# Attention block on one core: the places of the bias additions, of the weight split's test, of the residual loads and of the range test

## The chip, the cores and the metric

The kernel runs on one core of a Trainium2 chip. The metric is the time of one execution on the device in microseconds (us). A core has five engines, each with an instruction queue of its own that it works through in order: TensorE (PE in a profile, with its weight loads apart as PEld), VectorE (DVE), ScalarE (ACT), GpSimd (POOL) and SyncE (SP), which here only issues DMAs.

## The reference

```python
def reference(x, gn_scale, gn_bias, qkv_w, qkv_b, proj_w, proj_b):   # x: (4, 512, 48, 48) float32
    hn = group_norm(x, 32 groups) * gn_scale + gn_bias
    qkv = einsum('oc,bchw->bohw', qkv_w, hn) + qkv_b
    q, k, v = qkv as float16, 8 heads of 64 channels, 2304 positions
    w = softmax(einsum('bhct,bhcs->bhts', q * s, k * s))             # s = 64 ** -0.25 in float16
    a = einsum('bhts,bhcs->bhct', w, v)
    return x + einsum('oc,bchw->bohw', proj_w, a) + proj_b
```

## The kernel before

The function `fast_path` does the whole computation. A general version follows it behind a flag, and runs only if the sums of the softmax left a safe range or if the split of the projection weights was not exact; with these inputs it does not run. All engines' orders are written out by hand: the Python code emits instructions in exactly the order in which each engine's queue holds them.

Heads are worked on in pairs, 4 pairs for each of 4 images, 16 pairs `g` in all. Positions of the queries fall into 5 blocks `j`, four of 512 and one of 256. The list `stream` cuts this into 432 bursts, 27 for a pair (6, 6, 6, 6, 3 for the blocks). The main loop `for n in range(end)` emits burst `n`:

- `prepare(n)`: SP's transfers for the bias additions (below).
- `scores`: six matmuls into three two-bank tiles `ps`, and an `Exp` of ScalarE on each, which writes the tile `p`.
- `add(stream[n-1])`: VectorE adds the `p` of the burst before to the float16 sum `acc`. At the last burst of a block two or three smaller additions, the joins (L1184), fold `acc` together.
- `values(stream[n-BEHIND])`: matmuls of `v` with the `p` of two bursts ago into `av`; at a block's end VectorE copies `av` out (`avx`).
- `fill(n)`: work beside the attention. It runs VectorE tasks from the deque `tasks` (statistics `st` and normalization L776 of the next image) up to a budget `room`, and then pieces from the list `beside`: chains of matmuls that make `q`, `k` (tile `pqk`), `v` (`pv`) and the output projection (`pr`). A chain comes whole or in two halves in two bursts. One PSUM bank (`pw`) serves all chains, so that a chain begins once VectorE has copied the chain before out of it (L833, L882, L1032). The first chain on the next image's `v` waits in the list until block 0 of that image has been normalized in an earlier burst (`when`).

After a block's end at burst `e`, the sums are added up over partitions by PE (`sl`, L1207, into the bank that `av` had) at `e+3` and copied out (`slx`), inverted at `e+4` (`invert`), spread by DMA through DRAM at `e+5` (`spread`: `row`, `ib`), and multiplied with `avx` on POOL at `e+6` (`divide`, L1275). `check_sums` is the range test, four small operations of POOL on the sums at the end of a pair.

Four parts lie outside these chains:

- Bias additions. `fetch_x` loads a piece of `x` (256 KB, two buffers `pre`), `add_bias` adds the projection's bias on POOL two bursts later at the earliest (L946), `keep_biased` stores the piece in DRAM (`xb`) one burst after that. There are 72 pieces. `prepare` fetches one every second burst from burst 30 on, unless sums are being transferred or a projection chain is near.
- Residuals. `residual` loads a piece `xb` back (L925, four buffers `res`), and a projection chain's result is added to it on VectorE (L1032). The loads are issued `LEAD` chains ahead of the chain that uses them.
- The weight split. `split_wproj` splits each quarter of the projection weights into a high part `whi` and a float16 part `wlo` on VectorE; POOL compares what is left (L580, L581), and `test_split` reduces that on VectorE. They are pieces of `beside` between the chains of the first 16 bursts.
- `att32` copies attention results to float32 for the projection, some on ScalarE (L1002), some on POOL (L1000), as a piece just before the projection's chains.

Of the kernel before, what the change touches and what calls it, by code (L numbers as in the profile page):

```python
# [17 lines left out]
ALU = mybir.AluOpType  # L18
# [9 lines left out]
NC = C // P  # L28
# [5 lines left out]
BEHIND = 2  # L34
# [441 lines left out]
def fast_path(  # L476
# [12 lines left out]
    nc = tc.nc  # L489

    RES = NC
    LEAD = RES - 2
    FETCH_FROM, FETCH_EVERY = 30, 2
    const = ctx.enter_context(tc.tile_pool(name="const", bufs=1))
    xpool = ctx.enter_context(tc.tile_pool(name="xpool", bufs=1))
    qkp = ctx.enter_context(tc.tile_pool(name="qkp", bufs=3))
# [70 lines left out]
    wproj = {}  # L567
# [5 lines left out]
    def split_wproj(c):  # L573
        w = wproj[c]
        nc.vector.tensor_scalar(whi[:, c, :], w, UP, None, ALU.mult)
        nc.vector.scalar_tensor_tensor(
            w, w, UP, whi[:, c, :].bitcast(F32), ALU.mult, ALU.subtract
        )
        nc.vector.tensor_copy(wlo[:, c, :], w)
        nc.gpsimd.tensor_tensor(w, w, wlo[:, c, :], ALU.subtract)  # L580
        nc.gpsimd.tensor_scalar(w, w, 0.0, None, ALU.is_equal)  # L581

    def test_split(c):
        nc.vector.tensor_reduce(split_ok[:, c : c + 1], wproj.pop(c), AX.X, ALU.min)

    mhalf = const.tile([P, 2], F32, name="mhalf")
    nc.gpsimd.memset(mhalf, -0.5)
# [306 lines left out]
    now = [0]  # L894
# [34 lines left out]
    biased, heavy = {}, set()  # L929
    to_bias = deque((b, j, chunks) for b in range(B) for j, chunks in proj_list)  # L930
    fetched, added = deque(), deque()

    def fetch_x():
        b, j, chunks = to_bias.popleft()
        n = QBLOCKS[j][1]
        name = f"{b}_{j}_{chunks[0]}"
        t = work.tile([P, QB], F32, tag="pre", bufs=2, name=f"pre_{name}")
        t = t.rearrange("p (m n) -> p m n", n=n)
        nc.sync.dma_start(t, rows_of(x, b, j, chunks))
        fetched.append((now[0] + 2, (b, j, chunks), t))  # L940
# [12 lines left out]
        nc.sync.dma_start(kept, t)  # L953
        biased[b, j, chunks[0]] = kept

    fetch_at = [FETCH_FROM]

    def prepare(n):
        if added and added[0][0] <= n:
            keep_biased()  # L960
        transfers = block_at(n - BEHIND - 2) or block_at(n - BEHIND - 3)
        if any(id(p) in heavy for p in beside[:4]):
            fetch_at[0] = max(fetch_at[0], n + 2)
        elif to_bias and n >= fetch_at[0] and not transfers:
            fetch_x()
            fetch_at[0] = n + FETCH_EVERY

    def in_two(b, j):

# [320 lines left out]
    def put_run(run, *args, when=None, after=0):  # L1290

        put([piece(0.05, lambda: run(*args), when=when)], after)
# [27 lines left out]
    def do_tasks(room):  # L1320
        while tasks and tasks[0][0] <= now[0] and room > 0:
            if tasks[0][2] in powers and copies_next():
                break
            _, us, run = tasks.popleft()
            run()
            room -= us
# [50 lines left out]
    for b in range(B):  # L1377
        g = b * NPAIR
        old = b - 1
        if b == 0:  # L1380
            for j in range(NQ):
                if j < NC:
                    put_run(load_wproj, j)
                if j > 0:
                    put_run(split_wproj, j - 1)
                put_qk(g + 1, 1, (j,))
                put_qk(g + 1, 0, (j,))
                if 0 < j < NC:
                    put_run(test_split, j - 1)
            put_qk(g + 2, 1, (0,))  # L1390
            put_run(test_split, NC - 1)
            for block in SPARE:
                put_run(reload, *block)
        put_qk(g + 2, 1, range(0 if b else 1, NQ))
# [129 lines left out]
    def fill(n):  # L1524

        idle = beside and beside[0][4] and not beside[0][4]()
        if ended(n - 1):  # L1530
            room = 1.1 if idle else 0.0
        elif ended(n - BEHIND - 1) or ended(n - BEHIND - 2):
            room = 1.1 if idle else 0.5
        else:
            room = 2.4 if idle else 1.1
        do_tasks(room)
        rate, work = 0.0, 0.0
        for us, _, _, _, _, _, need in beside:
            work += us
            left = min(need * per_pair, len(stream) - 4) - n  # L1540
            rate = max(rate, work / max(left, 1))
        credit[0] = min(credit[0] + rate, 4.0)
        closed = False
        while beside:
            us, _, first, last, when, after, _ = beside[0]
            if after > n or (first and closed) or (when and not when()):
                break
            if us > 0.1 and credit[0] < (0.0 if first and last else us / 2):
                break
            issue()  # L1550
            closed = closed or last
# [17 lines left out]
    def block_at(n):  # L1569

        return stream[n][:2] if ended(n) and n not in soon else None
# [5 lines left out]
    for n in range(end):  # L1577
# [12 lines left out]
            load_due(n)  # L1590
        if inside:
            expect_end(kinds.DVE)
        if fetched and fetched[0][0] <= n and not block_at(n - BEHIND - 4):
            add_bias()
        if n > 0:
            add(stream[n - 1])
        filled = summed or n - BEHIND - 1 in soon
# [3 lines left out]
        if n >= BEHIND and not inside:  # L1601
            values(stream[n - BEHIND])
        if block_at(n - BEHIND - 2):
            check_sums(*block_at(n - BEHIND - 2))
            invert(*block_at(n - BEHIND - 2))
        if block_at(n - BEHIND - 3):
            spread(*block_at(n - BEHIND - 3))
# [2 lines left out]
            divide(*block_at(n - BEHIND - 4))  # L1610
        if not filled:
            fill(n)
        while joins:
            joins.popleft()()
        if n - BEHIND in soon:
# [153 lines left out]
```

## Time and profile before

| | us |
|---|---|
| median of 3 runs (lowest, highest) | 1591.56 (1590.95, 1591.70) |
| the profiled execution, its own time | 1593.29 |
| its span, first to last instruction | 1591.4 |
| PE busy | 1573.6 (99%) |
| ACT busy | 1269.0 (80%) |
| DVE busy | 1171.2 (74%) |
| POOL busy | 337.0 (21%) |

The span is what the trace covers; 1.9 us of the profiled execution lie around it, and this execution was 1.7 us longer than the median of the unprofiled runs. In rows of a timeline the first number is the start in us from the span's start, the second the length in us of the merged row, `x6` the number of instructions in it, and the bracket at the end the idle time of the engine before the row with what ended it. PE's ends are modelled: in a row of back-to-back matmuls the next row begins a little before the row's stated end.

### The profile page before, as it was taken

What the parts mean: (1) busy time and instruction counts of PE and PEld (TensorE: products, weight loads), DVE (VectorE), ACT (ScalarE), POOL (GpSimd) and SP (SyncE); (2) the same over time, 40 slices, a digit from 0 to 9 for tenths busy, and PEclk for the clock granted to TensorE, in tenths of its full rate; (3) what the DMA queues carried; (4) which work ended last, traced back from release to release, by engine and by line L of the source; (5) the groups of instructions that cost most, each with busy time, mean ns of one, the idle gap of its engine ahead of it and who ended that gap; (6) DMA issues with size and microseconds to landing.
All of it is one profiled execution on the core that took longest, in us unless ns stands there. A gap on an engine that the chain in (4) does not pass through costs nothing. (4 is left out here: it accounts for less than half of the span.)

```text
span 1591.4 us, 28818 instructions
## 1 busy us (share of the span) xinstructions
PE 1573.6 (99%) x11526; PEld 678.2 (43%) x11526; DVE 1171.2 (74%) x1302; ACT 1269.0 (80%) x1363; POOL 337.0 (21%) x297
## 2 busy tenths in 40 slices
PE   9999999999999999999999999999999999999997
PEld 3733434443333543445333354344533334434544
DVE  6277678877777668997766766889766666677786
ACT  4177777888888888888888888887878888888985
POOL 1041212213222222311322232211111001011313
PEclk9999999999999999999999999999999999999999
DMA  7002132211212225531122222453121000005514
GB/s 225 1 14 66 26 84 90 64 52 53 67 54 57 63 76 162 174 107 52 53 68 57 61 58 90 125 168 120 38 54 31 15 15 11 15 18 160 170 56 139
DMA packets 115633, 119.86 MB, mean 75 GB/s; under 512 B 53156, under 2 KB 63268, under 8 KB 115492
## 3 DMA queue, kind: packets, MB, share of 16 engines
q1 hardware_dynamic: 113460, 116.11, 25.0%
q8 instruction: 92, 1.51, 0.4%
q10 hardware_dynamic: 1904, 1.84, 0.4%
q14 instruction: 49, 0.40, 0.1%
q0 software_dynamic: 128, 0.01, 0.0%
HBM read 79.58 MB, written 38.04 MB: 74 GB/s over the span
## 5 line engine op out<-in xcount | busy, mean ns | idle before, releaser
L1130 ACT ACTIVATE p<-ps 128x1024 f16<-128x1024 f32 x1296 | 1233.4, 1025 | 294.8 <-PE ps L1123 290.4
L1179 DVE TENSOR_TENSOR acc<-acc,p 128x3072 f16<-128x3072 f16 x270 | 496.0, 1837 | 48.8 <-ACT p L1130 46.0
L822 PE MATMUL pqk<-x,wqkv 128*64 128x512 f32 (+1 forms) x2432 | 510.6, 549 | 1.9 <-DVE v L882 0.9
L1148 PE MATMUL av<-p,v 128*64 128x512 f16 (+1 forms) x2880 | 360.7, 364 | 0.0
L1123 PE MATMUL ps<-q,k 64*128 64x512 f16 (+1 forms) x2880 | 356.1, 358 | 0.5 <-DVE v L882 0.2
L1275 POOL TENSOR_TENSOR att<-avx,ib 128x512 f16<-128x512 f32 (+1 forms) x78 | 117.3, 1504 | 1009.0 <-DMA ib<-row 674.7
L874 PE MATMUL pv<-wqkv,x 128*64 128x256 f32 x2304 | 267.6, 379 | 1.0 <-DVE v L882 1.0
L822 PEld LDWEIGHTS pqk<-x,wqkv 128*64 128x64 f32 x2432 | 168.4, 137 | 208.1 <-issue 155.8
L1123 PEld LDWEIGHTS <-k 64*128 64x128 f16 x2880 | 106.7, 94 | 288.1 <-issue 238.8
L1148 PEld LDWEIGHTS <-v 128*64 128x64 f16 x2880 | 131.4, 109 | 211.4 <-issue 166.6
L874 PEld LDWEIGHTS pv<-wqkv,x 128*64 128x64 f32 x2304 | 166.2, 137 | 82.4 <-DVE v L882 2.0
L1179 DVE TENSOR_TENSOR acc<-p,p 128x3072 f16<-128x3072 f16 x79 | 139.9, 1772 | 0.0
L1184 DVE TENSOR_TENSOR acc<-acc 128x1024 f16<-128x1024 f16 x156 | 136.4, 874 | 3.3
L946 POOL TENSOR_TENSOR pre<-pre,bproj 128x512 f32<-128x512 f32 x72 | 115.1, 1613 | 22.3 <-DMA pre<-x_dram 21.7
L882 DVE TENSOR_TENSOR v<-pv,bv 128x512 f16<-128x512 f32 x72 | 49.6, 690 | 79.2 <-PE pv L874 79.0
L833 DVE TENSOR_SCALAR q<-pqk,bqkv 128x512 f16<-128x512 f32 (+1 forms) x77 | 53.4, 693 | 73.3 <-PE pqk L822 73.1
L833 DVE TENSOR_SCALAR k<-pqk,bqkv 128x512 f16<-128x512 f32 (+1 forms) x75 | 52.1, 694 | 70.9 <-PE pqk L822 70.9
L1223 DVE COPY slx<-sl 128x512 f32<-128x512 f32 (+1 forms) x79 | 50.6, 641 | 62.5 <-PE sl L1207 62.4
L1010 PE MATMUL pr<-a,whi 128*128 128x512 f32 (+1 forms) x311 | 93.5, 418 | 0.6 <-POOL a L1000 0.6
L1032 DVE SCALAR_TENSOR_TENSOR r<-pr,r 128x512 f32<-128x512 f32 x75 | 51.5, 687 | 38.8 <-PE pr L1010 34.4
L1010 PE MATMUL pr<-att,wlo 128*128 128x512 f16 (+1 forms) x311 | 75.1, 361 | 1.2 <-DVE r L1032 1.1
L1157 DVE COPY avx<-av 128x512 f32<-128x512 f32 (+1 forms) x79 | 50.4, 638 | 22.6 <-PE av L1148 22.1
(125 smaller groups left out, 477.7 us busy)
## 6 DMA issues: line engine op xcount, KB each, us to landing
pre<-x_dram SPq DMA_DIRECT2D x72, 256.0 KB, 3.5
xb<-pre SPq DMA_DIRECT2D x72, 256.0 KB, 3.2
r<-xb SPq DMA_DIRECT2D x72, 256.0 KB, 3.6
out_dram<-r SPq DMA_DIRECT2D x69, 256.0 KB, 2.6
ib<-row SPq DMA_DIRECT2D x126, 128.0 KB, 3.4
x<-x_dram SPq DMA_DIRECT2D x62, 256.0 KB, 4.3
x<-x_dram SPq DMA_DIRECT2D x16, 128.0 KB, 5.1
sums<-slx SPq DMA_DIRECT2D x128, 2.0 KB, 2.1
```

Of the source, the lines that this page charges most:

```text
L822: nc.tensor.matmul(pw[0][lo : lo + D, :n], wqkv[:, c, w0 + lo : w0 + lo + D], hn[b, c, j], start=(c == 0), stop=(c == NC - 1),)
L833: nc.vector.tensor_scalar(qk[g][part][:, o : o + n], pw[0][:, :n], bqkv[:, col : col + 1], SCALE, ALU.add, ALU.mult,)
L874: nc.tensor.matmul(pw[0][lo : lo + D, a, :], hn[b, c, i * P // QB][:, at + lo : at + lo + D], wqkv[:, c, 2 * C + half * C // 2 :][:, : C / ...
L946: nc.gpsimd.tensor_tensor(t, t, bias.to_broadcast(t.shape), ALU.add)
L1010: nc.tensor.matmul(ps[:, :n], w[:, bass.ts(m, P)], a, start=(i == 0), stop=(i == len(steps) - 1),)
L1032: nc.vector.scalar_tensor_tensor(xt, ps, DOWN, xt, ALU.mult, ALU.add)
L1123: nc.tensor.matmul(ps[:, h, a * n : (a + 1) * n], kt[rows, bass.ts(i, P)], qt[rows, o : o + n], start=True, stop=True,)
L1130: nc.scalar.activation(pt[:, r], ps, AF.Exp)
L1148: nc.tensor.matmul(av[0][lo : lo + D, :n], vv[b, pr // 2][:, i, pr % 2 * P + lo : pr % 2 * P + lo + D], pt[:, r, h, a * n : (a + 1) * n], ...
L1179: nc.vector.tensor_tensor(t, before, pt, ALU.add)
L1184: nc.vector.tensor_tensor(t[:, 0], t[:, 0], t[:, r], ALU.add)
L1275: nc.gpsimd.tensor_tensor(atts[g][:, o : o + n], avx.pop((g, j))[:, :n], ibs.pop((g, j))[:, :n], ALU.mult,)
```

## The change

`LEAD` goes from 2 to 3: each residual is loaded one chain earlier, into the same four buffers. The fetches for the bias additions begin at burst 8 in place of 30, come only in the two bursts after a block's end, and only while fewer than two pieces are in flight; an addition is emitted only in a burst that is not the first, second, third or sixth after a block's end, and in such a burst the VectorE tasks get a budget of at most 0.5. The comparison of the weight split goes from POOL (two operations) to VectorE (one), as a task together with its reduction. `check_sums` is emitted behind `fill`, and so behind the `att32` copies of the burst.

```diff
-    LEAD = RES - 2
-    FETCH_FROM, FETCH_EVERY = 30, 2
+    LEAD = RES - 1
+    FETCH_FROM = 8
 ...
     def split_wproj(c):
 ...
-        nc.gpsimd.tensor_tensor(w, w, wlo[:, c, :], ALU.subtract)
-        nc.gpsimd.tensor_scalar(w, w, 0.0, None, ALU.is_equal)
+        tasks.append((now[0] + 1, 0.69, lambda: compare_split(c)))
+        tasks.append((now[0] + 1, 0.68, lambda: test_split(c)))
+
+    def compare_split(c):
+        nc.vector.tensor_tensor(wproj[c], wproj[c], wlo[:, c, :], ALU.is_equal)
 ...
+    added_at = [-1]
 ...
-        transfers = block_at(n - BEHIND - 2) or block_at(n - BEHIND - 3)
-        if any(id(p) in heavy for p in beside[:4]):
-            fetch_at[0] = max(fetch_at[0], n + 2)
-        elif to_bias and n >= fetch_at[0] and not transfers:
-            fetch_x()
-            fetch_at[0] = n + FETCH_EVERY
+        after_end = ended(n - 1) or ended(n - BEHIND)
+        if to_bias and n >= FETCH_FROM and len(fetched) + len(added) < 2 and after_end:
+            if not transfers(n) and not any(id(p) in heavy for p in beside[:14]):
+                fetch_x()
+
+    def transfers(n):
+        return any(block_at(n - BEHIND - i) for i in (1, 2, 3))
+
+    def quiet(n):
+        return not any(ended(n - i) for i in (1, BEHIND, BEHIND + 1, BEHIND + 4))
 ...
-                if 0 < j < NC:
-                    put_run(test_split, j - 1)
             put_qk(g + 2, 1, (0,))
-            put_run(test_split, NC - 1)
+            put_run(splits_tested)
 ...
+        if added_at[0] == n:
+            room = min(room, 0.5)
         do_tasks(room)
 ...
-        if fetched and fetched[0][0] <= n and not block_at(n - BEHIND - 4):
+        if fetched and fetched[0][0] <= n and quiet(n):
             add_bias()
+            added_at[0] = n
 ...
         if block_at(n - BEHIND - 2):
-            check_sums(*block_at(n - BEHIND - 2))
             invert(*block_at(n - BEHIND - 2))
 ...
         if not filled:
             fill(n)
+        if block_at(n - BEHIND - 2):
+            check_sums(*block_at(n - BEHIND - 2))
```

First place, VectorE in bursts 12 to 14 (the third to fifth of the bursts around the end of block 1 of the first pair). `q_1` and `k_1` are copies out of the chains' bank, `whi`, `wproj` and `wlo` the split, `avx` and `slx` the copies of a block's end. Before:

```order
L833 TENSOR_SCALAR q_1_698<-pqk_1_0_3_1118,bqkv_98 128x512
L584 TENSOR_REDUCE tests_166<-wproj_2_891 128x1
L575 TENSOR_SCALAR whi_154<-wproj_3_1043 128x512
L576 SCALAR_TENSOR_TENSOR wproj_3_1043<-wproj_3_1043,whi_154 128x512
L579 CAST wlo_155<-wproj_3_1043 128x512
L1184 TENSOR_TENSOR acc_0_1_988<-acc_0_1_988 128x1024
L1157 COPY avx_0_1_1189<-av_0_1_999 128x512
L833 TENSOR_SCALAR k_1_699<-pqk_1_1_4_1191,bqkv_98 128x256
L1223 COPY slx_0_1_1228<-sl_0_1_1225 128x512
```

And now:

```order
L840 TENSOR_SCALAR q_1_698<-pqk_1_0_3_1116,bqkv_98 128x512
L575 TENSOR_SCALAR whi_154<-wproj_3_1041 128x512
L576 SCALAR_TENSOR_TENSOR wproj_3_1041<-wproj_3_1041,whi_154 128x512
L579 CAST wlo_155<-wproj_3_1041 128x512
L1194 TENSOR_TENSOR acc_0_1_987<-acc_0_1_987 128x1024
L1167 COPY avx_0_1_1188<-av_0_1_998 128x512
L584 TENSOR_TENSOR wproj_3_1041<-wproj_3_1041,wlo_155 128x512
L587 TENSOR_REDUCE tests_166<-wproj_3_1041 128x1
L840 TENSOR_SCALAR k_1_699<-pqk_1_1_4_1192,bqkv_98 128x256
L1233 COPY slx_0_1_1229<-sl_0_1_1226 128x512
```

The comparison and the reduction of a quarter now stand between `avx` and the copy of `k_1` out of the bank; before, a reduction stood ahead of the split and the comparison was POOL's.

Second place, VectorE in bursts 57 to 59, the end of the normalization of the second image's block 0 (`x_1_3_0` is its last quarter; `p_2_0_3`, `p_2_0_4` and `p_2_0_5` are the bursts' tiles). Before:

```order
L1179 TENSOR_TENSOR acc_2_0_2943<-acc_2_0_2943,p_2_0_2_2921 128x3072
L1255 RECIPROCAL inv_1_4_2988<-sums_1_170 128x2x2
L776 TENSOR_SCALAR x_1_3_0_2247<-x_1_3_0_2247,ga_1_2808,gb_1_2810 128x512
L833 TENSOR_SCALAR q_3_2168<-pqk_3_0_3_2946,bqkv_98 128x512
L1179 TENSOR_TENSOR acc_2_0_2943<-acc_2_0_2943,p_2_0_3_2962 128x3072
L776 TENSOR_SCALAR x_1_0_1_2355<-x_1_0_1_2355,ga_1_2808,gb_1_2810 128x512
```

And now:

```order
L1189 TENSOR_TENSOR acc_2_0_2952<-acc_2_0_2952,p_2_0_2_2930 128x3072
L1265 RECIPROCAL inv_1_4_3000<-sums_1_170 128x2x2
L783 TENSOR_SCALAR x_1_0_0_2267<-x_1_0_0_2267,ga_1_2957,gb_1_2959 128x512
L840 TENSOR_SCALAR q_3_2192<-pqk_3_0_3_2963,bqkv_98 128x512
L1189 TENSOR_TENSOR acc_2_0_2952<-acc_2_0_2952,p_2_0_3_2979 128x3072
L783 TENSOR_SCALAR x_1_1_0_2269<-x_1_1_0_2269,ga_1_2957,gb_1_2959 128x512
L1189 TENSOR_TENSOR acc_2_0_2952<-acc_2_0_2952,p_2_0_4_3020 128x3072
L783 TENSOR_SCALAR x_1_2_0_2271<-x_1_2_0_2271,ga_1_2957,gb_1_2959 128x512
L783 TENSOR_SCALAR x_1_3_0_2273<-x_1_3_0_2273,ga_1_2957,gb_1_2959 128x512
```

`x_1_3_0` is now normalized in burst 59, two bursts later. With it the first chain on the second image's `v`, `pv_1_0_0`, moved from bursts 58 and 59 (a half in each) to burst 60 (whole): PE's order of bursts 58 and 59 now holds scores and values and no chain. From there to about burst 267 the chains stand half a chain to a whole one later than before; no other burst is without a chain in either order, but for two at the very end that are the same in both.

Third place, POOL at burst 408, where the range test of the pair before and the copies for the third image's last projection block fall together. Before:

```order
L1275 TENSOR_TENSOR att_14_14442<-avx_14_3_15253,ib_14_3_15408 128x512
L1248 TENSOR_SCALAR in_14_4_15494<-sums_0_168 128x40
L1249 TENSOR_TENSOR tests_166<-tests_166,in_14_4_15494 128x40
L1248 TENSOR_SCALAR in_14_4_15497<-sums_0_168 128x40
L1249 TENSOR_TENSOR tests_166<-tests_166,in_14_4_15497 128x40
L1000 CAST a32_2_4_2_15518<-att_10_10663 128x256
```

And now:

```order
L1285 TENSOR_TENSOR att_14_14438<-avx_14_3_15251,ib_14_3_15406 128x512
L1010 CAST a32_2_4_2_15510<-att_10_10661 128x256
L1010 CAST a32_2_4_3_15512<-att_11_11764 128x256
L1010 CAST a32_3_3_2_15514<-att_14_14438 128x512
L1258 TENSOR_SCALAR in_14_4_15516<-sums_0_168 128x40
```

The copies now stand directly behind the product of the block before. For the additions themselves POOL's order changes little: in both versions two additions stand between two products L1275 of neighbouring blocks.

More of the change, by code (lines that the diff above doesn't have):

```diff
@@ L579, in split_wproj, with splits_tested @@
         nc.vector.tensor_copy(wlo[:, c, :], w)
-        nc.gpsimd.tensor_tensor(w, w, wlo[:, c, :], ALU.subtract)
-        nc.gpsimd.tensor_scalar(w, w, 0.0, None, ALU.is_equal)
+        tasks.append((now[0] + 1, 0.69, lambda: compare_split(c)))
+        tasks.append((now[0] + 1, 0.68, lambda: test_split(c)))
+    def compare_split(c):
+        nc.vector.tensor_tensor(wproj[c], wproj[c], wlo[:, c, :], ALU.is_equal)
     def test_split(c):
         nc.vector.tensor_reduce(split_ok[:, c : c + 1], wproj.pop(c), AX.X, ALU.min)
+    def splits_tested():
+        while wproj:
+            tasks.popleft()[2]()
     mhalf = const.tile([P, 2], F32, name="mhalf")
@@ L954, in keep_biased @@
         biased[b, j, chunks[0]] = kept
-    fetch_at = [FETCH_FROM]
     def prepare(n):
```

## The prediction, on record before the run

> **What bounds the kernel now.** I read the page's busy times and clock first, then its costliest groups, then the timeline of TensorE.
>
> ```profile
> span 1591.4 us, 28818 instructions
> PE 1573.6 (99%) x11526; PEld 678.2 (43%) x11526; DVE 1171.2 (74%) x1302; ACT 1269.0 (80%) x1363; POOL 337.0 (21%) x297
> PEclk9999999999999999999999999999999999999999
> ...
> L1130 ACT ACTIVATE p<-ps 128x1024 f16<-128x1024 f32 x1296 | 1233.4, 1025 | 294.8 <-PE ps L1123 290.4
> L1179 DVE TENSOR_TENSOR acc<-acc,p 128x3072 f16<-128x3072 f16 x270 | 496.0, 1837 | 48.8 <-ACT p L1130 46.0
> ...
> pre<-x_dram SPq DMA_DIRECT2D x72, 256.0 KB, 3.5
> xb<-pre SPq DMA_DIRECT2D x72, 256.0 KB, 3.2
> r<-xb SPq DMA_DIRECT2D x72, 256.0 KB, 3.6
> ```
>
> PE is busy 99% of the span at full granted clock in every slice, and the exponentials wait 294.8 us for PE: PE is the bound, and its work is untouched by the diff. So the change is worth the stalls of PE that it takes away, less those it makes. Nearly all sit ahead of a chain that wants its bank. This is the timeline of PE at the ones that count, the bracket being the wait, and below them an undisturbed piece:
>
> ```profile
> 103.26 0.41 PE L1207 MATMUL sl<-acc,ones 128*64 128x512 f16 x2 [0.58 <-DVE avx L1157]
> 103.92 1.54 PE L822 MATMUL pqk<-x,wqkv 128*64 128x512 f32 x6 [0.25 <-DVE k L833]
> ...
> 125.45 0.41 PE L1207 MATMUL sl<-acc,ones 128*64 128x512 f16 x2 [0.24 <-DVE avx L1157]
> ...
> 277.98 1.51 PE L822 MATMUL pqk<-x,wqkv 128*64 128x512 f32 x6 [0.93 <-DVE v L882]
> ...
> 289.79 0.82 PE L1123 MATMUL ps<-q,k 64*128 64x512 f16 x6
> 290.54 0.84 PE L1148 MATMUL av<-p,v 128*64 128x512 f16 x6
> 291.21 1.89 PE L874 MATMUL pv<-wqkv,x 128*64 128x256 f32 x16
> 293.04 0.82 PE L1123 MATMUL ps<-q,k 64*128 64x512 f16 x6
> ...
> 297.04 0.84 PE L1148 MATMUL av<-p,v 128*64 128x512 f16 x6
> 297.71 3.62 PE L874 MATMUL pv<-wqkv,x 128*64 128x256 f32 x32
> ...
> 323.43 1.95 PE L874 MATMUL pv<-wqkv,x 128*64 128x256 f32 x16 [0.87 <-DVE v L882]
> ...
> 609.37 1.94 PE L822 MATMUL pqk<-x,wqkv 128*64 128x512 f32 x8 [0.64 <-DVE k L833]
> ...
> 1049.14 1.02 PE L1010 MATMUL pr<-att,wlo 128*128 128x512 f16 x4 [0.80 <-DVE r L1032]
> ...
> 1503.51 0.73 PE L1010 MATMUL pr<-a,whi 128*128 128x256 f32 x2 [0.62 <-POOL a L1000]
> ```
>
> Undisturbed, a values row of 0.84 is followed after 0.67 (290.54 to 291.21) and a scores row of 0.82 after 0.75 (289.79 to 290.54). The loss at a stall is thus the bracket plus 0.17 or 0.07, up to 0.24 where two brackets follow each other: 1.07 at 103, 0.46 at 125 (0.31 there, and 0.15 more behind the two matmuls), 1.10 at 277, 1.04 at 323, 0.81 at 609, 0.87 at 1049 and about 0.8 at 1503. Together 6.1 us: more than that the change cannot gain.
>
> **Weight split.** VectorE and POOL at the first place:
>
> ```profile
> 98.44 2.60 POOL L580 TENSOR_TENSOR wproj<-wproj,wlo 128x512 f32<-128x512 f32 x1 [6.44 <-DVE wlo L579]
> 100.06 2.54 DVE L1184 TENSOR_TENSOR acc<-acc 128x1024 f16<-128x1024 f16 x2
> ...
> 122.00 0.67 DVE L584 TENSOR_REDUCE tests<-wproj 128x1 f32<-128x512 f32 x1
> ...
> 125.32 0.47 DVE L833 TENSOR_SCALAR k<-pqk,bqkv 128x256 f16<-128x256 f32 x1
> ```
>
> The two joins take 2.54 beside POOL's comparison. With POOL out they need about 1.3, and the 1.07 falls to about 0.45, as at the second place: -0.6 (bounds -1.07 and 0). At the second place the order now puts comparison and reduction between `avx` and the copy of `k`. VectorE loses the reduction ahead (0.67) and gains, at this place, the reduction and a comparison, which the trace does not show on VectorE (I take 0.65, nearest to the reduction of the same 512 elements; the ends are 0.47, the shortest row here, and 1.3, half the joins' 2.54). The copy then starts near 125.32 - 0.67 + 0.67 + 0.65 = 125.97, and PE, whose next work in order is that chain, waits 0.65 longer: +0.65 (bounds 0, if the copy's own input is late anyway, and 1.3).
>
> **Range test.** POOL before the copies for the last chains:
>
> ```profile
> 1500.28 0.32 POOL L1248 TENSOR_SCALAR in<-sums 128x40 f32<-128x40 f32 x1
> ...
> 1503.07 1.29 POOL L1000 CAST a<-att 128x256 fp32r<-128x256 f16 x3
> ```
>
> The four test operations stand for 2.8 us ahead of the copies. Behind them they delay no one: the next product is some bursts off, and POOL is 21% busy. The stall goes: -0.8 (bounds -0.8 and 0).
>
> **Residuals.** The stall at 1049 bears VectorE's name, yet the row of VectorE shows that it waited itself:
>
> ```profile
> 1048.39 0.69 DVE L1032 SCALAR_TENSOR_TENSOR r<-pr,r 128x512 f32<-128x512 f32 x1 [1.42 <-PE av L1148]
> ```
>
> PE had its values and the chain done before. On SP's queue the load of that residual stands late:
>
> ```profile
> 1043.68 0.42 SPq L925 DMA_DIRECT2D r<-xb  x1
> ```
>
> From 1043.68 to 1048.39 are 4.7 us, against 3.6 from issue to landing in the page's median: the addition started when its load came. One chain more of lead is several us; the transfer is early: -0.87 (bounds -0.87 and 0). With four buffers and three in front, a load must wait until the chain before has been stored from its buffer, and everything behind it on SP waits along; there is a chain's length for that, and I cost it at nothing.
>
> **Additions.** VectorE at the three stalls, POOL at two:
>
> ```profile
> 273.70 1.04 POOL L946 TENSOR_TENSOR pre<-pre,bproj 128x512 f32<-128x512 f32 x1
> 273.79 2.57 DVE L1179 TENSOR_TENSOR acc<-p,p 128x3072 f16<-128x3072 f16 x1
> ...
> 318.04 2.40 POOL L946 TENSOR_TENSOR pre<-pre,bproj 128x512 f32<-128x512 f32 x2
> 319.46 2.59 DVE L1179 TENSOR_TENSOR acc<-acc,p 128x3072 f16<-128x3072 f16 x1
> ...
> 605.49 2.57 DVE L1179 TENSOR_TENSOR acc<-p,p 128x3072 f16<-128x3072 f16 x1
> ```
>
> An addition to `acc` that meets one on POOL takes 2.6 against the page's mean of 1.84, which has the slow ones in it, and the copy out of the bank behind it on VectorE is late by that, some 0.8. The pair at 605 is of the same kind: its row has the same length, and PE's stall follows it. The two at 318 stand in the order in bursts 67 and 69 but ran back to back, straight after a product: POOL has no clock, only an order and its releasers. An addition runs when its piece has landed and POOL is free, whatever burst the code emitted it in. What paces it is SP:
>
> ```profile
> 311.41 0.41 SPq L953 DMA_DIRECT2D xb<-pre  x1
> ...
> 313.95 1.01 SPq L939 DMA_DIRECT2D pre<-x_dram  x2
> ```
>
> In the new order a fetch must follow the store that frees its buffer. With a store at 311.4 landing 3.2 later, the fetch goes at 314.6, lands 3.5 later at 318.1, and the next about 2.5 behind it: 318 to 321 again, in a block's last burst and the first of the next, not in the quiet ones. So the quiet-burst rule does not hold in time. What changes is which work stands beside it, since the bursts have shifted: I take 1.1 (at 277), 0.8 (at 609) and half of 1.04 (at 323) as gone, -2.4 of 2.95 (bounds -2.95 and 0), and one new meeting of the size of 609, +0.8 (bounds 0 and 2.95). The cap of 0.5 on tasks costs directly nothing, since VectorE is 74% busy; what it costs by order is the next term.
>
> **Bursts without a chain.** In the new order a quarter's normalization comes two bursts later, and bursts 58 and 59 hold no chain. Now they are the bursts that begin at 289.79 and 293.04, and each holds half of one; the whole chain at 297.71 takes 3.62 and the half 1.89, so that a half adds 1.73 to a burst. Without a chain ScalarE then sets the pace:
>
> ```profile
> 290.28 2.86 ACT L1130 ACTIVATE p<-ps 128x1024 f16<-128x1024 f32 x3 [0.44 <-PE ps L1123]
> ```
>
> Six exponentials back to back end at 290.28 + 5 x 0.92 + 1.02 = 295.9 (1.02 is the page's mean for one, and 2.86 for three then means a pitch of 0.92). The third pair of the next scores follows on that tile and ends near 296.15, against 297.04 now: 0.89 sooner. The two halves are done later and cost 2 x 1.73 = 3.46 there. Net +2.57 (bounds 0, if the chains get going earlier than listed, and 3.46).
>
> **Sum.** -0.6 + 0.65 - 0.8 - 0.87 - 2.4 + 0.8 + 2.57 = -0.65. The profiled execution took 1593.29, of which the span is 1591.4; it stands 1.7 above the median of 1591.56. I put the difference on the median: 1590.9. Differences under 0.2%, 3.2 us, cannot be told from none.
>
> **Rivals.** *All additions come clear and the gap is cheap:* the terms become -0.6 + 0.65 - 0.8 - 0.87 - 2.95 and, if the hole's chain is caught up, 0: -4.6, or 1587.0. For it: seven stalls of one kind of cause are named. Against: SP's rows put the additions where they were. Chance 0.22.
>
> *Later chains meet the block's end:* from burst 60 to about 267 chains stand half a chain to a whole one later, so a copy out of the bank comes at other places relative to the joins, `avx` and the tasks. At 125 a copy behind `avx` already costs 0.46; if five of the some 35 block ends in that stretch pay about 0.8, the sum is -0.65 + 4 = 1595; from four on the change is slower than before. VectorE's 74% speaks for it, since a copy may stand behind several tasks; against it, that the chains now lie as close to other block ends and only six such stalls show. Chance 0.13.
>
> *The clock drops in the empty bursts:* two gaps of about 1.3 us follow each other there (ScalarE's 2.86 for a burst against PE's 0.75 + 0.67 without a chain). The windows show this stretch now, and the end of the kernel:
>
> ```profile
> 290.00:301.40 11.40, 11.40 (x102) 5.89 (x100) 9.40 (x12) 8.57 (x9) 4.17 (x5) 1.00 0.21 59
> 1580.00:1592.00 12.00, 2.54 (x16) 1.40 (x14) 4.81 (x10) 0.41 (x1) 3.85 (x5) 0.78 0.46 160
> ```
>
> The granted clock (third from last) is 1.00 here, and 0.78 only where PE works 2.54 of 12.00 us; the stalls of 1.1 in the middle left every slice of the clock at 9. If the gaps did halve it for one burst of 3.25 (289.79 to 293.04), the sum is -0.65 + 3.25: 1594.2. Chance 0.07. [...]
>
> *Nothing moves:* the additions meet what they met, and the empty bursts cost little: about 1591.5. Chance 0.08. That leaves 0.5 for the forecast.
>
> **Range and chances.** Low end: the first rival, 1587.0; high end: the second, 1595.0. Faster by over 0.2% (under 1588.4): the 0.22 of the first rival and a little of the forecast's spread, 0.24. Slower (over 1594.7): most of the second's 0.13 and little of the clock's, 0.14. Else 0.62. The forecast's own range is 1589.3 to 1593.
>
> **What would show it.** PE's brackets gone at 1049 and 1503 and shrunk at 103; a bracket of about 0.9 at 125; exponentials without a wait for two bursts near 290 and PE waiting for ScalarE there; L946 rows still behind products and beside additions to `acc`. I am wrong if the additions fall into the quiet bursts in time, if new waits for VectorE appear between 300 and 1000, or if the granted clock falls below 1.00 near 295.

## The result, and the profile after

| | before | after |
|---|---|---|
| median of 15 runs, us | 1591.64 | 1594.89 |
| ratio, 95% interval | | 1.0021 (1.0013 to 1.0029) |
| profiled execution, its own time | 1593.29 | 1593.84 |
| its span | 1591.4 | 1592.1 |

The changed kernel is 0.2% slower, 2 to 4.6 us by the interval; one of its 15 runs, at 2270.05 us with a granted clock of 0.654, is left out of the ratio. The forecast was 1590.9. The direction was wrong, though the time lies in the range of 1587.0 to 1595.0, close to its upper end; it lies outside the forecast's own 1589.3 to 1593. The two first profiles hardly show it: the profiled execution of before stands 1.65 over its median, that of after 1.05 under its own. So both kernels were profiled again, below. From the page of after:

```profile
span 1592.1 us, 28851 instructions
PE 1573.0 (99%) x11526; PEld 679.3 (43%) x11526; DVE 1163.7 (73%) x1306; ACT 1268.9 (80%) x1364; POOL 310.0 (19%) x288
PEclk9999999999999999999999999999999999999999
...
L1140 ACT ACTIVATE p<-ps 128x1024 f16<-128x1024 f32 x1296 | 1233.2, 1026 | 295.3 <-PE ps L1133 291.9
L1189 DVE TENSOR_TENSOR acc<-acc,p 128x3072 f16<-128x3072 f16 x270 | 493.9, 1829 | 43.2 <-ACT p L1140 40.4
```

TensorE is the bound as before, with the digit 9 for its clock in every slice and a mean granted clock of 0.998. `acc` takes a mean of 1829 ns in place of 1837; by my estimate from these means the additions on POOL meet it nearly as often as before. The waits are in other places. TensorE's timeline of after, the main rows with a wait:

```profile
103.09 1.97 PE L829 MATMUL pqk<-x,wqkv 128*64 128x512 f32 x8 [0.51 <-DVE k L840]
...
126.25 1.98 PE L829 MATMUL pqk<-x,wqkv 128*64 128x256 f32 x16 [1.31 <-DVE k L840]
...
291.53 0.39 PE L1133 MATMUL ps<-q,k 64*128 64x512 f16 x2 [0.52 <-ACT p L1140]
292.45 0.39 PE L1133 MATMUL ps<-q,k 64*128 64x512 f16 x2 [0.52 <-ACT p L1140]
...
294.28 0.39 PE L1133 MATMUL ps<-q,k 64*128 64x512 f16 x2 [0.35 <-ACT p L1140]
295.20 0.39 PE L1133 MATMUL ps<-q,k 64*128 64x512 f16 x2 [0.52 <-ACT p L1140]
...
320.11 1.95 PE L881 MATMUL pv<-wqkv,x 128*64 128x256 f32 x16 [0.30 <-DVE v L889]
...
605.05 1.94 PE L829 MATMUL pqk<-x,wqkv 128*64 128x512 f32 x8 [0.59 <-DVE q L840]
...
678.71 1.02 PE L1020 MATMUL pr<-att,wlo 128*128 128x512 f16 x4 [0.30 <-DVE r L1042]
```

Counted as in the prediction (start to start, less the undisturbed distance) these are 0.68 at 103, 1.47 at 126 (the place called 125 below), 2.56 in the four waits for ScalarE, 0.47 at 320, 0.76 at 605 and 0.36 at 679. The stalls at 277, 609, 1049 and 1503 are gone.

The first bursts show a collision that the prediction had not looked for, since the fetches now begin at burst 8. Timeline of VectorE and POOL, after:

```profile
114.84 4.82 DVE L1189 TENSOR_TENSOR acc<-acc,p 128x3072 f16<-128x3072 f16 x2
115.53 5.02 POOL L954 TENSOR_TENSOR pre<-pre,bproj 128x512 f32<-128x512 f32 x2
...
123.80 0.68 DVE L1167 COPY avx<-av 128x512 f32<-128x512 f32 x1
124.40 0.68 DVE L584 TENSOR_TENSOR wproj<-wproj,wlo 128x512 f32<-128x512 f32 x1
125.11 0.69 DVE L587 TENSOR_REDUCE tests<-wproj 128x1 f32<-128x512 f32 x1
125.72 0.47 DVE L840 TENSOR_SCALAR k<-pqk,bqkv 128x256 f16<-128x256 f32 x1
...
598.72 1.77 POOL L1285 TENSOR_TENSOR att<-avx,ib 128x512 f16<-128x512 f32 x1 [17.81 <-DMA ib<-row]
599.40 3.16 DVE L1194 TENSOR_TENSOR acc<-acc 128x1024 f16<-128x1024 f16 x2
600.97 1.04 POOL L954 TENSOR_TENSOR pre<-pre,bproj 128x512 f32<-128x512 f32 x1 [0.48 <-POOL att L1285]
...
603.08 1.27 DVE L651 BATCH_NORM_STATS2 st<-x 128x6 f32<-128x512 f32 x2
604.27 0.73 DVE L840 TENSOR_SCALAR q<-pqk,bqkv 128x512 f16<-128x512 f32 x1
```

Two `acc` take 4.82 beside two additions of 5.02; in split_only below, where no addition runs at this place, the same two take 4.15. At 124.40 comparison and reduction stand ahead of the copy of `k`, as predicted. At 603.08 two statistics stand ahead of the copy of `q` in the second burst after a block's end. Ahead of them the two joins take 3.16 beside a product and an addition on POOL; at 99.04, with POOL idle, two joins take 1.42. So order and a meeting with POOL both make this copy late, and no run here parts them.

### The profile page after: what moved, and what is told of

Read it like the earlier page. It is cut to its first block, busy times and chain, and to the rows that moved or that the text cites. A ratio compares the mean times of both kernels' runs of the same rounds, so it can differ in the third digit from the quotient of the medians.

```text
span 1592.1 us, 28851 instructions
## 1 busy us (share of the span) xinstructions
PE 1573.0 (99%) x11526; PEld 679.3 (43%) x11526; DVE 1163.7 (73%) x1306; ACT 1268.9 (80%) x1364; POOL 310.0 (19%) x288
## 5 line engine op out<-in xcount | busy, mean ns | idle before, releaser
L1189 DVE TENSOR_TENSOR acc<-acc,p 128x3072 f16<-128x3072 f16 x270 | 493.9, 1829 | 43.2 <-ACT p L1140 40.4
L1285 POOL TENSOR_TENSOR att<-avx,ib 128x512 f16<-128x512 f32 (+1 forms) x78 | 121.2, 1554 | 1108.6 <-DMA ib<-row 910.6
L1194 DVE TENSOR_TENSOR acc<-acc 128x1024 f16<-128x1024 f16 x156 | 129.1, 828 | 3.5
L954 POOL TENSOR_TENSOR pre<-pre,bproj 128x512 f32<-128x512 f32 x72 | 102.0, 1423 | 39.4 <-DMA pre<-x_dram 35.7
```

The source lines that it names most:

```text
L954: nc.gpsimd.tensor_tensor(t, t, bias.to_broadcast(t.shape), ALU.add)
L1189: nc.vector.tensor_tensor(t, before, pt, ALU.add)
L1194: nc.vector.tensor_tensor(t[:, 0], t[:, 0], t[:, r], ALU.add)
L1285: nc.gpsimd.tensor_tensor(atts[g][:, o : o + n], avx.pop((g, j))[:, :n], ibs.pop((g, j))[:, :n], ALU.mult,)
```

## Experiments

All medians of one group ran on the same chip beside runs of the kernel before. For each profile the table gives the profiled execution's time; the part from the first exponential of the attention to the first one of the last burst ("middle"); TensorE's stalls between 73 and 1565 us, counted as above; and the part from the end of the flag operation to the end of the span ("end").

| profile | its time | middle | stalls | end |
|---|---|---|---|---|
| before | 1593.29 | 1500.07 | 8.0 | 5.95 |
| before_again | 1591.54 | 1498.96 | 7.4 | 5.58 |
| after | 1593.84 | 1500.01 | 7.9 | 7.13 |
| after_again | 1594.62 | 1501.44 | 9.3 | 6.51 |
| after_c | 1594.33 | 1501.29 | 9.2 | 6.27 |
| no_cap | 1591.14 | 1497.58 | 5.8 | 6.63 |
| split_late | 1594.39 | 1500.78 | 8.8 | 6.49 |
| gap_only | 1598.87 | 1503.95 | 11.5 | 6.11 |
| split_only | 1591.53 | 1497.87 | 6.1 | 6.49 |
| lead_check | 1592.51 | 1498.95 | 6.9 | 6.28 |
| pad | 1592.23 | 1499.18 | 7.7 | 6.17 |
| adds_only, adds_b, adds_c | 1589.87, 1589.77, 1592.72 | 1496.68, 1496.60, 1498.74 | 5.1, 5.3, 6.7 | 6.22, 6.15, 6.86 |
| adds_lead | 1592.02 | 1498.82 | 6.4 | 6.31 |
| mended | 1589.66 | 1495.37 | 4.3 | 7.36 |
| spread_last | 1588.31 | 1494.50 | 3.4 | 6.65 |
| lead2 | 1593.60 | 1500.31 | 7.4 | 6.39 |

**Both kernels again.**

> The kernel before, unchanged, for a second profile. Theory A (the stalls at 277, 323 and 609 are there in every execution, and what made the changed kernel 3.25 us slower is what it adds): the profile shows the same stalls of TensorE, 8.0 us between 73 and 1565 as before, and the stretch from the last flag operation (DVE flag) to the end of the span is 6.05 us. Rival B (the first profile of before was a bad draw, 1.7 us over the median: the collisions of additions with acc come and go): one or more of 277, 323 and 609 is gone, the sum of stalls is nearer 6.3, and so the change had less to take away than its profile showed.

> The changed kernel, unchanged, for a second profile. Theory A: the gap of two bursts near 290 (2.57 us of waits) and the stall of 1.47 at 125 are there again, the sum of stalls between 73 and 1565 is 7.9 again, and the stretch after the flag is 7.2 us again (three engines fetch the code behind the branch later than in before), time about 1594.9. Rival B: the stalls by additions differ from the first profile (319, 604), and the stretch after the flag varies by more than 0.5.

> The changed kernel, a third profile. The gap's four waits, the stalls at 102 and 125, those at 604 and 678, and SP and ScalarE beginning over 3 us after the branch: all there again, mid part 1500.0 to 1501.5. Rival: one of them is missing, so that it belongs to a draw and not to the kernel.

Before: 1591.64, ratio 0.9997 (0.9988 to 1.0007), which tells what the method resolves. After: 1594.78, ratio 1.0019 (1.0009 to 1.0029). In before the stalls at 277 and 322 (1.09, 1.03) were there again and that at 608 fell from 0.81 to 0.10, that at 1503 was gone, so theory A and rival B both hold in part. In after everything named came back three times (125: 1.47 each time; gap: 2.56 each time; 605: 0.75 to 0.77; 679: 0.36), with others that come and go, such as 0.53 at 437, or 0.24, 0.29 and 1.29 at 301. Between the two executions near their medians, before_again and after_again, the middle grew by 2.48 and the end by 0.93, of 3.08 in all.

**The gap of two bursts.** `no_cap` takes two lines out of after:

```diff
-        if added_at[0] == n:
-            room = min(room, 0.5)
```

> The changed kernel without the cap of 0.5 on VectorE's tasks in a burst with an addition, so that the normalization ends where it did before and no burst is without a chain. Theory A (the gap costs its full 2.57): 1594.9 - 2.6 = 1592.3, the waits for ScalarE near 290 gone. Rival C (the gap is caught up by shifted chains, and the loss is in other bursts): 1594.9 as before, with as much stalls elsewhere. Rival D (additions now collide more, since the cap protected the chains): over 1594.

1591.16, ratio 0.9996 (0.9987 to 1.0006): 3.6 less than after_again in the same group, more than the 2.56 of the waits. Against before in its group it is 0.6 faster, which is not told apart from no change. Its profile has none of the four waits near 290 and none of the stalls at 605 and 679. `gap_only` puts the gap alone into before:

```diff
-        while beside:
+        while beside and n not in (58, 59):
```

> The kernel before, with nothing changed but that no chain may be issued in bursts 58 and 59; TensorE's order is then that of the changed kernel, row for row. Theory A (the gap costs 2.57 by itself and moves the chains behind it so that copies at 604 and 678 come late): the waits for ScalarE near 290 as in the changed kernel, the stalls of 0.7 at 604 and 0.36 at 678 appear, 1591.7 + 2.6 + 1.0 = 1595.3. Rival E (the stalls at 604 and 678 are made by the moved additions): they do not appear, 1591.7 + 2.6 = 1594.3. Rival C (the gap is made up later): 1591.7.

1595.37, ratio 1.0028 (1.0017 to 1.0039), 4.0 over before in its group, as theory A had it. TensorE's timeline of gap_only:

```profile
293.75 0.39 PE L1123 MATMUL ps<-q,k 64*128 64x512 f16 x2 [0.52 <-ACT p L1130]
...
322.04 1.95 PE L874 MATMUL pv<-wqkv,x 128*64 128x256 f32 x16 [0.30 <-DVE v L882]
...
606.94 1.51 PE L822 MATMUL pqk<-x,wqkv 128*64 128x512 f32 x6 [0.52 <-DVE q L833]
...
681.68 1.02 PE L1010 MATMUL pr<-att,wlo 128*128 128x512 f16 x4 [0.36 <-DVE r L1032]
```

The stalls at 605 and 679 follow the gap without any of the additions' rules: rival E falls. The wait at 322 is down to 0.30 here too, so after owes that gain to the shifted chains. The stall at 277, ahead of the gap, is there with 1.10. The profiled execution of gap_only, 3.5 over the median, lost 1.6 of that before its first exponential (74.88 against 73.25 in before_again), where the granted clock was 0.50 for 3.4 us (last section).

**The weight split.** `split_late` (in after) and `split_only` (in before, the split's lines of the diff alone):

```diff
-        tasks.append((now[0] + 1, 0.69, lambda: compare_split(c)))
-        tasks.append((now[0] + 1, 0.68, lambda: test_split(c)))
+        tasks.append((now[0] + 2, 0.69, lambda: compare_split(c)))
+        tasks.append((now[0] + 2, 0.68, lambda: test_split(c)))
```

> The changed kernel with the comparison and the reduction of a split quarter allowed one burst later, so that they stand behind the copy of k out of the bank at the second place. Theory A: the stall of 1.47 at 125 falls to about 0.45 and nothing else moves: 1594.9 - 1.0 = 1593.9. Rival: the comparison and the reduction hold up the next copies in bursts 14 and 15 instead, and the time stays 1594.9.

> The kernel before with the weight split's part of the change alone. Theory A (comparison and reduction stand ahead of the copy of k at both places): the stall at 103 falls from 1.07 to 0.68, that at 125 rises from 0.46 to 1.47, no stall at 122: 1591.7 + 0.6 = 1592.3. Rival: the comparison takes the time of POOL's without delaying k, 1591.3. If the longer stretch behind the flag (6.5 to 7.1 against 5.6 to 5.95) goes with POOL's fewer instructions, it shows here, and the time is 0.9 more.

split_late: 1594.39, ratio 1.0017 (1.0007 to 1.0026), 0.4 less than after_again. The 1.47 fell to 0.15, but a stall of 0.99 stands at 122, which in after is 0.1 to 0.3. VectorE in split_late:

```profile
116.84 1.76 DVE L584 TENSOR_TENSOR wproj<-wproj,wlo 128x512 f32<-128x512 f32 x1
118.64 0.69 DVE L587 TENSOR_REDUCE tests<-wproj 128x1 f32<-128x512 f32 x1
...
122.48 0.74 DVE L840 TENSOR_SCALAR q<-pqk,bqkv 128x512 f16<-128x512 f32 x1
```

The moved comparison and reduction of the quarter before now stand between two `acc`, and the comparison takes 1.76 beside the early additions on POOL (0.68 elsewhere). So the copy of `q` behind them is late, much as the rival had it though at another copy, and more than half of the gain went there. split_only: 1592.27, ratio 1.0007 (0.9997 to 1.0016); 0.68 and 1.12 in place of 1.07 and 0.46, and nothing at 122. So without the early additions the split costs 0.66 at 125, as forecast, and 0.35 of the 1.47 in after came with them. Its time is the expected one but not told apart from no change; its end is 6.49, so the last condition of its expectation was met too.

**Residuals and range test.** `lead_check` is before with these two edits of the diff.

> The kernel before with LEAD of 3 and the range test behind the copies, nothing else. Theory A: the stall at 1047 (0.86 and 0.93 in two profiles) is gone, and that near 1503, which was there in one of two profiles of before (0.6), cannot come: 1591.7 - 0.9 - 0.3 = 1590.5. Rival: loads one chain earlier wait on SP's queue for a buffer and hold up the transfers behind them, 1591.7 or more.

1591.94, ratio 1.0005 (0.9996 to 1.0014): no gain. The stall at 1048 is gone, and one of 0.91 stands at 1542. This one varies: 0 to 0.80 in nine profiles with LEAD of 2, 0.32 to 1.12 in nine with 3. How it looks in mended, on SP and VectorE:

```profile
1533.06 0.37 SPq L1268 DMA_DIRECT2D row<-inv  x1
1533.47 1.42 SPq L933 DMA_DIRECT2D r<-xb  x3
```

```profile
1538.79 0.69 DVE L1043 SCALAR_TENSOR_TENSOR r<-pr,r 128x512 f32<-128x512 f32 x1 [2.86 <-DMA r<-xb]
```

Three loads go out at once behind a `row`, and VectorE waits 2.86 for the first to land, 5.3 after its issue. The stall at 1048 varies as well: 0 to 0.93 in the nine profiles with `LEAD` of 2, none in the nine with 3.

**Additions alone.** Before with the new rules for fetches and additions, without the cap and from burst 18; `adds_lead` has `LEAD` of 3 besides.

> The kernel before with the new rules for fetches and additions alone, without the cap, and from burst 18; TensorE's order is that of before, row for row. Theory A (the additions leave acc alone at 277, 322 and 608): these stalls fall from 1.09, 1.03 and 0.1 to 0.8 to 0.3 and less each, -2.0; SP has 1269 instructions ahead of the branch like the changed kernel's 1264, so +0.9 behind the flag: 1591.5 - 2.0 + 0.9 = 1590.4. Rival F (the argument of the prediction that POOL runs additions when they have landed, so that the rules change nothing by themselves): the three stalls stay, 1592.4.

> The kernel with the additions' rules alone, a second profile. Open: its mid part was 2.3 us under that of before in the first profile, which was its fastest execution (1589.87), yet its median (1591.65) is that of before. Theory J (late residual loads with LEAD of 2 cost some executions 1 to 4 us, by a stall and by half the clock behind it): 1591 to 1593, with a stall of over 0.9 ahead of a projection chain and VectorE waiting for r, or with a stretch of clock 0.5. Theory K (the additions meet acc again in most executions): stalls of 1.0 at 277 or 322 or 608 are back.

> The same kernel, a third profile. Theory J: stalls ahead of projection chains that wait for r differ from profile to profile, those at 277, 322 and 608 stay at 0.3 or less. Theory K: the reverse.

> The additions' rules with LEAD of 3. Theory J: the slow executions go, 1591.65 - 1.0 = 1590.6, and no stall over 0.9 before a projection chain. Theory K: as without, 1591.6.

adds_only: 1591.65, ratio 1.0004 (0.9995 to 1.0013). In its three profiles the stalls at 277, 322 and 608 were 0.27, 0.18 to 0.31 and 0.12 or less. VectorE in adds_only at the first of them:

```profile
273.52 1.75 DVE L1182 TENSOR_TENSOR acc<-p,p 128x3072 f16<-128x3072 f16 x1
...
276.15 0.68 DVE L882 TENSOR_TENSOR v<-pv,bv 128x512 f16<-128x512 f32 x1
```

`acc` is back at 1.75 and the copy of `v` 1.1 sooner than in before. On POOL, from 262 to 282, nothing is left that adds a bias:

```profile
261.23 2.03 POOL L1278 TENSOR_TENSOR att<-avx,ib 128x512 f16<-128x512 f32 x1 [13.40 <-DMA ib<-row]
272.76 0.72 POOL L667 TENSOR_TENSOR rstd<-veps,mhalf 128x2 f32<-128x2 f32 x1 [9.50 <-DVE both L670]
```

So rival F, the argument of the prediction, falls at 277: the rules alone, with TensorE's order unchanged, take the addition away. At 322 it holds for POOL, where two additions still run from 318.4; but VectorE begins its `acc` there 1.2 to 2.4 sooner than in before, and the stall is small in all three profiles. What separates adds_b from adds_c (2.1 in the middle) are stalls in other places: 0.58 at 808, 0.71 at 1047 and 0.57 at 1502, among smaller ones, against 0.79 at 1541 in adds_b and 0.41 in adds_c. So K falls for these kernels and J explains the spread in part. But adds_lead, 1591.00, ratio 0.9999 (0.9989 to 1.0008), had 1.03 at 322 in its profile: with another lead the collision is back (`acc` takes 2.59 at 318); that this comes from other landing times is likely and not shown. That the median of adds_only did not follow the 2 us of its stalls is settled only in part: 0.4 to 1.1 of it went to the end of the kernel (next; 6.15 to 6.86 against a mean of 5.77 in before), the rest is within the interval.

**The end.** `pad` adds to before, at the head of a burst:

```diff
+        if 340 <= n < 340 + 33:
+            extra = dram.tile([1, 1], F32, tag=f"extra_{n}", bufs=1, name=f"extra_{n}")
+            nc.sync.dma_start(extra, ones[0:1, 0:1])
+        if 340 <= n < 340 + 5:
+            nc.gpsimd.memset(spare[:, n - 340 : n - 339], 0.0)
```

> The kernel before with 33 transfers of 4 bytes on SP's queue and five settings of one element on POOL, spread over bursts 340 to 372, where both engines idle; nothing waits for them. Theory G (the longer stretch behind the flag in the changed kernel comes from where SP's and POOL's code lies when the branch at the end jumps over the general version): TensorE's stalls as before, mid part near 1499, but SP begins again 3.2 to 4.2 after its branch in place of 1.9, POOL 4.0 to 4.3 in place of 3.0 to 3.4, ScalarE 1.0 as before; the stretch is 6.5 to 7.1 in place of 5.6 to 5.95, time 1592.4. Rival: the stretch goes with what the changed kernel does at its end, and stays at 5.6 to 5.95, time 1591.5.

The view of one source line shows the branch that jumps over the general version and the semaphore operation that is each engine's first behind it (count, shortest, median and longest ns, first and last start). Before:

```profile
L1730 SPq EVENT_SEMAPHORE  x8: 17/17/17, 1588.6 to 1589.1; - x8
L1730 SPq COMPARE_BRANCH  x1: 70/70/70, 1586.7 to 1586.7; - x1
...
L1730 ACTq EVENT_SEMAPHORE  x1: 17/17/17, 1587.8 to 1587.8; - x1
L1730 POOLq EVENT_SEMAPHORE  x1: 17/17/17, 1590.1 to 1590.1; - x1
```

And in after:

```profile
L1742 SPq EVENT_SEMAPHORE  x8: 17/17/17, 1590.0 to 1590.5; - x8
L1742 SPq COMPARE_BRANCH  x1: 70/70/70, 1586.0 to 1586.0; - x1
...
L1742 ACTq EVENT_SEMAPHORE  x1: 17/17/17, 1590.2 to 1590.2; - x1
L1742 POOLq EVENT_SEMAPHORE  x1: 17/17/17, 1590.3 to 1590.3; - x1
```

SP goes on 1.9 after its branch in before and 4.0 in after. In before POOL is the last to go on, at 1590.1, and the closing semaphore operations of ScalarE, VectorE and TensorE start together behind that, at 1590.8; in after SP's run of semaphore operations, to 1591.2, ends last, and they start at 1591.5. In pad:

```profile
L1736 SPq EVENT_SEMAPHORE  x8: 17/17/17, 1588.4 to 1588.9; - x8
L1736 SPq COMPARE_BRANCH  x1: 70/70/70, 1585.4 to 1585.4; - x1
...
L1736 ACTq EVENT_SEMAPHORE  x1: 17/17/17, 1586.6 to 1586.6; - x1
L1736 POOLq EVENT_SEMAPHORE  x1: 17/17/17, 1588.7 to 1588.7; - x1
```

SP's delay rose from 1.9 to 3.0 with 36 more instructions on its queue (1231 to 1267) and nothing else changed on it; ScalarE's stayed near 1.1 and POOL's at 3.3, which I had expected at 4. The end is 6.17, between the two expectations, and the time of 1592.25, ratio 1.0007 (0.9998 to 1.0016), is not told apart from no change. Over the profiles SP's delay goes with its count of instructions ahead of the branch, and not evenly: 3.2 at 1229 (split_only), 1.8 to 1.9 at 1231, 0.5 at 1233 and 1235 (gap_only, lead_check), 3.0 to 4.2 from 1264 on. For ScalarE no pad was run, but the profiles divide cleanly: 0.7 to 1.2 in all whose program has 1856 instructions of it ahead of the branch, 3.4 to 3.8 in all with 1854. That for SP the position of the code is behind this is my estimate from the pad and these counts. But the pad is one profile, the same program's delay was 3.0 to 4.0 in three profiles of after, and that this is the whole of the 0.9 between the ends is not shown. Between 1586.9 and 1587.5 in after, 0.9 to 1.5 behind SP's branch, five transfers of instructions start on the DMA queues; in before four start between 1586.9 and 1588.0, 0.3 to 1.3 behind it. So these transfers do not show what the expectation of after_again has, that three engines fetch the code behind the branch later; what the traces show is that SP, ScalarE and POOL go on later, 4.0, 3.8 and 4.3 after their branches in place of 1.9, 1.1 and 3.4.

**A mended version.** After without the cap, and:

```diff
-    FETCH_FROM = 8
+    FETCH_FROM = 18
 ...
-        tasks.append((now[0] + 1, 0.69, lambda: compare_split(c)))
-        tasks.append((now[0] + 1, 0.68, lambda: test_split(c)))
+        at = now[0] + (1, 3, 1, 2)[c]
+        tasks.append((at, 0.69, lambda: compare_split(c)))
+        tasks.append((at, 0.68, lambda: test_split(c)))
```

> The changed kernel without the cap, with the fetches from burst 18 in place of 8 (behind the last quarter of the split), and with the comparison and reduction of quarters 1 and 3 one or two bursts later, so that they stand behind the copies of k. Theory A (stalls of 5.8 us in the kernel without the cap, of which 0.68 at 102, 0.53 at 122 and 1.47 at 125 go, but for some 0.2 left): 1591.2 - 2.5 = 1588.7, faster than the kernel before by 3.0. Rival: a VectorE that is as full meets the additions elsewhere, 1591.

> The mended kernel with the transfer of a block's inverted sums (row) issued behind the burst's chain work instead of ahead of it, so that residual loads of that burst do not stand behind it on SP's queue. Theory H (with LEAD of 3 the three loads at 1533 stood behind a row that waited for VectorE, and landed late: the stall of 1.12 at 1538): the stall falls to 0.3 or less and the time to 1589.4 - 0.8 = 1588.6. Rival: the product att, which needs the row, comes late instead, 1589.4 or more.

> The mended kernel with LEAD back at 2. Theory H (LEAD of 3 gains the stall near 1047 and loses about as much near 1540): the stall at 1538 falls from 1.12 to 0.35, one of about 0.9 near 1035 to 1045 appears, 1589.4 within 0.3. Rival (LEAD of 3 is worth the 0.87 of the prediction): 1590.3.

The last two edits:

```diff
-        if block_at(n - BEHIND - 3):
-            spread(*block_at(n - BEHIND - 3))
 ...
             fill(n)
+        if block_at(n - BEHIND - 3):
+            spread(*block_at(n - BEHIND - 3))
```

```diff
-    LEAD = RES - 1
+    LEAD = RES - 2
```

mended: 1589.38, ratio 0.9987 (0.9978 to 0.9996). The stalls at 102, 122 and 125 are all gone; its end is 7.36, or the gain would be larger. spread_last: 1588.44, ratio 0.9982 (0.9973 to 0.9991), the lowest median here; its interval overlaps those of the two others, so it is not told apart from them. Theory H would not be its reason: on SP the row still stands ahead of the three loads, and the stall is 0.69. lead2: 1589.69, ratio 0.9988 (0.9979 to 0.9998); about 0.7 near 1048 came, as expected, but 0.80 at 1543 stayed, where 0.35 was expected. Its profiled execution, the slowest of its runs at 1593.60, shows what a late residual can cost. TensorE and VectorE, and then the windows around (busy time of the engines, PE first; the granted clock stands third from last):

```profile
673.74 0.69 DVE L1043 SCALAR_TENSOR_TENSOR r<-pr,r 128x512 f32<-128x512 f32 x1 [2.51 <-DMA r<-xb]
...
674.48 1.86 PE L1021 MATMUL pr<-att,wlo 128*128 128x512 f16 x4 [2.24 <-DVE r L1043]
```

```profile
671.00:674.40 3.40, 1.24 (x12) 0.35 (x7) 0.89 (x3) 3.29 (x5) 1.26 (x2) 0.99 0.40 148
674.40:677.80 3.40, 3.32 (x8) 1.72 (x7) 2.14 (x5) 0.00 (x0) 0.00 (x0) 0.50 0.46 155
677.80:690.00 12.20, 12.20 (x77) 5.35 (x78) 10.94 (x14) 10.12 (x13) 0.74 (x2) 1.00 0.53 145
```

## Why the prediction was wrong, step by step

The step that failed is the sum. It took gains at the full size that one execution showed, and it put at nothing what comes behind the gap and what happens at the end of the kernel. `no_cap` parts this in two. Without the gap the forecast's terms add up to -3.2; `no_cap` measured -0.6 against before (-2.1 to +1.0 by its interval). The gap was forecast at +2.57; the cap, and with it the gap, cost 3.6. In that group the change is +3.0, and of the 3.7 between this and the forecast 2.6 lie in the gains and the end, and 1.0 behind the gap.

- **What bounds.** Right. The sum of stalls decided, and the forecast of one more or less per place was the right account.
- **Bursts without a chain.** +2.57 was forecast, 2.56 measured: the mechanism and the size were right. What failed is what came behind it: the prediction made the shifted chains a rival at 0.13, with five meetings at 0.8, and gave them nothing in the sum. There were two that are there every time, 0.76 at 605 and 0.36 at 679, and with them came the sign that it named for being wrong, new waits for VectorE between 300 and 1000. The gap and its shift cost 3.6 (no_cap) to 4.0 (gap_only), against the 2.57 in the sum. That the time came out near the 1595 of that rival is luck: 1.1 of its 4 us came.
- **Weight split.** At the second place +1.01 against +0.65: the copy started at 125.72, close to the 125.97 forecast, but TensorE came 0.4 earlier. split_only has +0.66 there; the rest came with the early additions. At the first place -0.39 against -0.6, since comparison and reduction stand ahead of `k` there too, which I had not read in the order.
- **Additions.** That most additions run outside the quiet bursts was right: in each of three profiles of after 14 of 72 fell into the fourth and fifth burst of a block, none in before. The reason given for the gain, that the bursts have shifted, was wrong at the largest stall. 277 went whole (-1.1, as forecast), yet it lies ahead of the gap: gap_only, which has the shift alone, keeps it, and adds_only, which has the rules alone, loses it. So the number was right by luck. 323 went by half, but in after through the gap. 609 gave way to 605. What was missed: beginning at burst 8 puts two additions beside `acc` at 115 and costs 0.1 to 0.3 at 122, 0.35 at 125, and a part of the 0.99 in split_late.
- **Range test.** -0.8 was priced from one profile. The stall was in one of three profiles with the same order up to the pads (before, before_again, pad), so it is worth 0.2 to 0.3 on the mean.
- **Residuals.** The 0.87 at 1049 went in every profile of after, but loads that pile up near 1540 took some 0.3 back; "I cost it at nothing" was wrong for SP's queue. lead_check, which has this edit and the range test alone, shows no gain: +0.6, or -0.6 to +2.2 by its interval. So the 0.9 taken for both below rests on the stalls and not on a time.
- **Not in the sum at all.** The end of the kernel, 0.9 on the mean of the profiles (5.77 to 6.64).

With these sizes: +3.7 (gap and shift), +0.3 (split), +0.5 (early additions), -0.3 (range test), -0.6 (residuals), -1.7 (277 and 323 by half; 609's own stall, 0.5 on the mean of before, before_again and pad, is set against 0.2 to 1.3 at 301 in after), +0.9 (end): +2.8, against 3.25 between the medians. This sum was made after the result, from stalls of a few profiles. The gap's part is shown by taking it out and by putting it in alone; the other parts are each within what the method resolves.

Of the rivals, the clock did not drop in the gap: TensorE worked on in it, 2.35 and 2.53 of 3.40 us in its two halves, and the clock stayed at 1.00. The half clock that this rival put into its sum is granted in the trace of before only behind the end of TensorE's work (0.50 from 1588.2 to 1591.4); that a gap of two bursts could bring it about no run shows.

## What to carry to other kernels

Sort the stalls of a trace by whether the order fixes them or the landing of a transfer does; the second kind came and went between executions here (0 to 0.93 at 1048 in nine profiles, against 1.47 at 125 in each of three), so price it below its size and take two profiles before betting on it. The hole in the bound engine's order cost its 2.56 here, and 3.6 to 4.0 with what it moved behind it: check the copies out of the bank at the next blocks' ends. A cap that guards a small collision may delay what other work waits for; look at the whole order for a stretch in which the bound engine has nothing.

## What was not expected of the hardware

- Behind one stall the clock halved: in lead2 TensorE worked 1.24 of 3.40 us, with a stall of 2.24, and the next 3.40 us ran at 0.50. In the gap of after it worked more of the time, 2.35 and 2.53 of 3.40 us with four waits of 0.35 to 0.52, and kept 1.00. The share of busy time alone does not tell the two apart: near the start of gap_only's profiled execution 0.50 was granted behind a window with 2.38 of 3.41 us busy by PE's modelled ends, more than the 2.35 that kept 1.00 in the gap of after. Its windows, columns as above:

```profile
7.60:11.01 3.41, 2.38 (x14) 1.29 (x14) 2.39 (x10) 2.58 (x5) 0.58 (x1) 1.00 1.09 346
11.01:14.42 3.41, 3.41 (x10) 1.14 (x10) 3.26 (x10) 2.10 (x3) 0.02 (x1) 0.50 1.06 382
```

- SP went on between 0.5 and 4.2 us after the last branch over these kernels, at the end of programs that do the same work. The delay goes with the count of SP's instructions ahead of the branch, and not evenly: 3.2 at 1229, 0.5 at 1233 and 1235, 1.8 to 1.9 at 1231, 3.0 to 4.2 from 1264 on. That the place of the code is behind it is my estimate from these counts.
